# Layer 0's experts on sorted tokens: rows fetched by indirect DMA, weights addressed from a register

## The chip, the core and the metric

The kernel runs on one core of a Trainium2 chip. The metric is the device time of one execution in microseconds. A core has TensorE (PE, with its weight loads shown apart as PEld), VectorE (DVE), ScalarE (ACT), GpSimd (POOL) and SyncE (SP), which here only issues transfers; the transfers of all queues run on 16 DMA engines.

## What is computed

The reference is a decoder of two layers on 32 sequences of 128 tokens with 128 features, all float32. Layer 0 has a time-mixing block, self attention and cross attention with 16 heads of 64, a feed-forward with 512 hidden features, and a mixture of experts; layer 1 has an attention, a cross attention with a mask, and a second mixture of experts with a capacity. Each block's output goes through a layer normalization. The change is about layer 0's experts:

```
t = x * rsqrt(mean(x*x) + 1e-6) * norm_weight
gate_logits = t @ gate_w.T                       # 8 experts
gate_scores, expert_idx = top_k(gate_logits, 2)
routing_weights = softmax(gate_scores)
combine = zeros(T, 8).at[arange(T)[:, None], expert_idx].add(routing_weights)
for each expert (W1, B1, W2, B2, c = its column of combine):
    acc += c[:, None] * (gelu(t @ W1.T + B1) @ W2.T + B2)    # 128 -> 256 -> 128
out = x + acc
```

Every token thus uses two of the eight experts; the other six have a weight of zero. The layer's result is the normalization of x + out.

## The kernel before

The 4,096 tokens are cut into eight groups of 512 (G = 4 sequences). Between layers a group's rows go out to DRAM and come back (`putx`, `getx`, L174 to L186). Each layer is written as units, and `build` (L1361) places every piece of work at a time measured in units; `pipeline` sorts the pieces by that time, and the framework then orders each engine's instructions from this list by a simulated timeline of its own. `SHIFT`, `AHEAD`, `FC`, `L5`, `L6` and so on (L26 to L57) are those due times. Layer 0's cross attention runs from unit 64 to 135, the feed-forward (`fc_parts`, L527) of a group starts eleven units ahead of its experts, the experts run from unit 132 to 203, and layer 1's attention starts at unit 172.

Buffers are shared by tag (`BUFS` and `TAG`, L34 to L40): a tag has a few slots, and all uses that name it, of whatever layer, take turns in them. So `x` has four slots, `xs` four, `cs` five, `res` two, `pt` four, `e` six. PSUM's eight banks are shared in the same way (`BANKS`).

The experts (`moe_units`, L629) treat a group as a whole, with no regard to the choice of experts. `pre` normalizes the rows (Square on ScalarE, L642; the power on POOL, L646; scaling on VectorE, L648), transposes them and splits the result into a high and a low part (L652, L653). `route` computes the logits, the two best experts as one-hot rows (`top2`, L571) and the weights. `hid(e)` multiplies all 512 tokens with expert e's first matrix, as three rounded products for each half (`mm3`, L149, recorded at L152 to L154) and a Gelu (L694). `outp(e)` multiplies with the second matrix in plain float32 (L705) and adds the result, times the token's weight for this expert, to an accumulator on VectorE (L708). `turn_c` and `post` add the second biases by one small matmul a sequence (L680, L714, L717). All weights stay in SBUF (`moe_w`, L618).

Beside the experts run the loads for layer 1's experts: `presplit` (L1128) takes a slab through one staging buffer (SP's load at L1134, a cast on ScalarE at L126, a subtraction on POOL at L127) and writes it back from POOL's queue (L1136). Layer 1's attention has its own work on POOL (`rope` at L865, `parts3` at L739 to L742), on VectorE (L862, L903) and on ScalarE (L930).

Of the kernel before, what the change touches and what calls it, by code (L numbers as in the profile page):

```python
# [9 lines left out]
F32 = mybir.dt.float32  # L10
FR = mybir.dt.float32r
# [11 lines left out]
G = 4  # L23
GT = G * 128

SHIFT = {1: 0, 2: 0, 3: 4, 4: 0, 5: -24, 6: 8, 7: 0}  # L26
# [10 lines left out]
           mt="res", acc="xb", ct8="msk", mh="v", mres="res", parts="qk", stack="big", ob="v", ax="cs", at="pt", ar="pt",  # L37
           ap="e", ok="pt", ares="cs", oT="v", xwo="pt", mi="xb", m="msk", cx="xs", cc="v", xt="pt", xr="v", xp="e",
           xres="cs", pre="big", turn="xs", turnw="v", kT="xs", kh="x", kl="cs", hot="xs", d="big", w="e", hh="e", hl="qk",
           w2="pt", eo="big", kres="v", mx0="xs", mx1="cs", s0="msk", s1="xb", x="x")  # L40
# [3 lines left out]
            oproj="mm", fc1="mm", fc2="S", logits="mm", logitsT="PT", cT="PT", hid="mm", outp="S", b2="PT", bank="PV",  # L44
# [10 lines left out]

AHEAD = {2: 8, 3: 32, 4: 24, 5: 20, 6: 40, 7: 164}
# [13 lines left out]
class Net:  # L70
# [546 lines left out]

    def moe_w(self):  # L618
        w = {}
        w["w1"] = [self.split_slab("moe_w1", i * 1024) for i in range(2)]  # L620
        w["w2"] = None
        w["b1"] = self.col("moe_b1", 16)
        w["nw"] = self.col("moe_nw", 1)
        w["g"] = self.gate_w("moe_gate")
        w["b2"] = self.cst.tile([8, 128], F32, name="moe_b2")
        self.nc.sync.dma_start(out=w["b2"], in_=self.a["moe_b2"])
        return w

    def moe_units(self, g, getw, done):  # L629
        nc, sm = self.nc, self.sm  # L630
        w = Later(getw)
        st = {}

        def load():
            st["x"] = self.getx(g)

        def pre():
# [9 lines left out]
            for b in range(G):  # L647
                nc.vector.tensor_scalar(t[:, b, :], x[:, b, :], rs[:, b:b + 1], None, ALU.mult)  # L648
            tp = self.xT_ps(t)
            th = self.t("mx1" if g % 2 else "mx0", dt=FR)  # L650
            tl = self.t("mx1" if g % 2 else "mx0", dt=FR)
            nc.scalar.activation(th, tp, AF.Copy, scale=w["nw"])  # L652
            nc.vector.scalar_tensor_tensor(tl, tp, w["nw"], th.bitcast(F32), ALU.mult, ALU.subtract)  # L653
            st["t"] = th, tl
            acc = self.tok("acc")
            nc.gpsimd.tensor_tensor(acc, x, x, ALU.add)
            st["acc"] = acc

        def route():
            lg = sm.tile([128, G, 8], F32, name="lg")  # L660
            self.logits(w["g"], *st["t"], lg)
            (o1, o2), (m1, m2) = self.top2(lg)
            d = sm.tile([128, G], F32, name="d")
            nc.vector.tensor_tensor(d, m1, m2, ALU.subtract)
            th = sm.tile([128, G], F32, name="th")
            nc.scalar.activation(th, d, AF.Tanh, scale=0.5)
            p = sm.tile([128, 2, G], F32, name="p")
# [869 lines left out]
```

## Time and profile before

| what | us |
|---|---|
| median of 2 runs | 1868.26 (1867.07 to 1869.44) |
| profiled execution, its own time | 1872.84 |
| its span in the profile | 1871.1 |
| ScalarE busy, 670 to 940 us | 195.52 of 270 |
| VectorE busy, 940 to 1243 us | 211.84 of 303 |
| TensorE busy, 1600 to 1871 us | 244.29 of 271 |

A group of instructions is shown as: line, engine, operation, output and input by name, shapes and count, then busy time and the mean ns of one, then the engine's idle time ahead of them and what ended it. Since matmuls overlap, the mean of one is longer than the step from one to the next; the steps are read from the chain of waits, which lists the work that ended last in order of time. The profile takes one execution; times beside each other are compared within it, and the medians between kernels.

### The profile page before, as it was taken

Reading aid. Unit: us, or ns where it says so; the run is one execution under the profiler, and the core shown is the slowest. Engines: PE = TensorE matmul, PEld = TensorE weight load, DVE = VectorE, ACT = ScalarE, POOL = GpSimd, SP = SyncE. Lnnn points to the kernel's source line nnn. Section 1 sums busy time; section 2 is a strip of 40 time slices with the busy share of each in tenths; the row PEclk is TensorE's granted clock in tenths of the full one; section 3 lists DMA queues with packets and bytes.
Section 4 is the critical chain, followed back from the end, with each engine's and each line's share of the span. In section 5 each row is a group of like instructions: output and inputs, shape, how many; then the busy total and the mean of one; then the engine's idle time right before and its main releaser. Section 6 shows DMA issues by size and latency. Waiting matters only on the chain.

```text
span 1871.1 us, 44846 instructions
## 1 busy us (share of the span) xinstructions
PE 1728.4 (92%) x15658; PEld 1400.8 (75%) x15658; DVE 1383.4 (74%) x5256; ACT 1177.4 (63%) x3703; POOL 863.3 (46%) x1201
## 2 busy tenths in 40 slices
PE   5899999989999999999999999999779888898998
PEld 3677777777778788887788888866556555688888
DVE  7978888776766676666776677677655767789896
ACT  2776766768777777777645554346666646556654
POOL 4655555564544444444434444245432432246555
PEclk7999999999999999999999999999998989899999
DMA  5101101010110000100133435468979988222222
GB/s 158 36 31 40 39 20 41 31 53 26 48 48 26 20 13 25 42 8 12 57 119 123 164 134 130 109 179 198 200 191 225 217 197 205 73 81 92 96 90 70
DMA packets 148770, 171.45 MB, mean 92 GB/s; under 512 B 13128, under 2 KB 100176, under 8 KB 146064
## 3 DMA queue, kind: packets, MB, share of 16 engines
q1 hardware_dynamic: 145808, 154.95, 31.0%
q0 software_dynamic: 1584, 11.54, 1.5%
q8 instruction: 124, 2.03, 0.5%
q10 hardware_dynamic: 1152, 2.10, 0.3%
q14 instruction: 102, 0.84, 0.1%
HBM read 114.81 MB, written 55.31 MB: 91 GB/s over the span
## 4 chain that ended last, share of the span: by engine, by line
PE 62%; DVE 18%; ACT 6%; DMA 5%; POOL 4%; issue 3%; SPq 1%; POOLq 0%; ACTq 0%; DVEq 0%
PE mm L489 6%; PE S L705 6%; PE mm L152 6%; PE mm L153 5%; PE mm L154 5%; PE PV L169 4%; PE PT L452 4%; PE S L169 3%; DVE e L432 3%; PE PV L164 3%; PE PT L1283 3%; ACT e L437 2%; DMA x<-x 2%; PE S L164 2%; PE S L554 2%
## 5 line engine op out<-in xcount | busy, mean ns | idle before, releaser
L437 ACT ACTIVATE e<-e,nm 128x128 f32<-128x128 f32 x1024 | 397.6, 391 | 108.5 <-POOL nm L434 106.4
L441 POOL TENSOR_TENSOR e<-e,ri 128x512 f32<-128x512 f32 x256 | 266.1, 1044 | 205.0 <-DVE ri L439 185.7
L432 DVE CUSTOM_DVE_ANT_0 e<-S,msk 128x128 f32<-128x128 f32 x1024 | 228.7, 284 | 21.5 <-PE PT L452 12.8
L437 ACT ACTIVATION_READ_ACCUMULATOR e<-e,nm 128x1 f32 x1024 | 193.1, 189 | 0.0
L452 PE MATMUL PT<-ident,e 128*128 128x128 f32 x1024 | 150.8, 278 | 6.8 <-ACT v L397 4.6
L169 PE MATMUL S<-qk 64*128 64x128 f32 x1792 | 148.5, 280 | 0.0
L169 PE MATMUL PV<-pt,v 128*64 128x128 f32 x1792 | 141.1, 277 | 0.0
L452 PEld LDWEIGHTS PT<-ident,e 128*128 128x128 f32 x1024 | 115.6, 141 | 32.7 <-issue 8.7
L694 ACT ACTIVATE v<-mm,col_moe_b 128x512 f32<-128x512 f32 x128 | 85.5, 685 | 81.8 <-PE mm L154 81.3
L705 PEld LDWEIGHTS S<-w,v 128*128 128x128 f32 x1024 | 128.6, 191 | 7.8
L705 PE MATMUL S<-w,v 128*128 128x128 f32 x1024 | 133.7, 276 | 0.0
L152 PE MATMUL mm<-xs,w 128*128 128x512 f32 x296 | 127.2, 441 | 4.7 <-DVE qk L409 1.9
L489 PE MATMUL mm<-w,big 128*128 128x128 f32 x1024 | 127.6, 278 | 0.0
L489 PEld LDWEIGHTS mm<-w,big 128*128 128x128 f32 x1024 | 120.9, 192 | 7.6 <-issue 5.0
L439 DVE RECIPROCAL ri<-su 128x4 f32<-128x4 f32 x256 | 43.4, 173 | 110.7 <-ACT e L437 106.4
L169 PEld LDWEIGHTS S<-qk 64*128 64x128 f32 x1792 | 123.9, 188 | 0.4 <-DVE x L220 0.4
L153 PE MATMUL mm<-xs,w 128*128 128x512 f32 x296 | 118.9, 402 | 1.6 <-DVE xs L146 1.6
L434 POOL TENSOR_SCALAR nm<-mx 128x4 f32<-128x4 f32 x256 | 58.6, 233 | 133.1 <-DVE mx L432 119.5
L154 PE MATMUL mm<-xs,w 128*128 128x512 f32 x296 | 118.4, 400 | 0.0
L230 POOL TENSOR_SCALAR rsqv<-bmv 128x4 f32<-128x4 f32 (+1 forms) x73 | 14.4, 197 | 214.4 <-DVE bmv L203 197.7
L454 ACT COPY pt<-PT 128x512 f32<-128x512 f32 x128 | 74.3, 581 | 59.5 <-PE PT L452 58.8
L169 PEld LDWEIGHTS PV<-pt,v 128*64 128x64 f32 x1792 | 108.7, 137 | 2.3 <-issue 2.2
(324 smaller groups left out, 5052.1 us busy)
## 6 DMA issues: line engine op xcount, KB each, us to landing
x<-x SPq DMA_DIRECT2D x151, 256.0 KB
big<-d_st SPq DMA_DIRECT2D x52, 512.0 KB
pt<-d_w SPq DMA_DIRECT2D x64, 256.0 KB
d_st<-qk SPq DMA_DIRECT2D x48, 256.0 KB
d_st<-qk SPq DMA_DIRECT2D x16, 768.0 KB
d_w<-big POOLq DMA_DIRECT2D x11, 1024.0 KB, 5.1
w<-d_w SPq DMA_DIRECT2D x7, 1024.0 KB
w<-d_st SPq DMA_DIRECT2D x12, 512.0 KB
```

What stands on the lines that cost most here:

```text
L152: mm(out=out, lhsT=wh, rhs=xh, start=True, stop=False)
L153: mm(out=out, lhsT=wh, rhs=xl, start=False, stop=False)
L154: mm(out=out, lhsT=wl, rhs=xh, start=False, stop=True)
L164: i = mm(out=out, lhsT=w, rhs=x, **more)
L169: i = mm(out=out, lhsT=w, rhs=x, **more)
L432: self.seen = nc.vector.tensor_tensor_reduce(e[:, t], s[h][:, t], msk[:, t], 1.0, NEG, ALU.add, ALU.max, mx[:, b:b + 1])
L437: nc.scalar.activation(e[:, t], e[:, t], AF.Exp, bias=nm[:, b:b + 1], scale=0.125, accum_out=su[:, b:b + 1])
L441: nc.gpsimd.tensor_tensor(e3, e3, ri.unsqueeze(2).to_broadcast([128, G, 128]), ALU.mult)
L452: nc.tensor.transpose(pt[:, t], es[h][:, t], self.ident)
L489: nc.tensor.matmul(out=o[:, b, :], lhsT=st["ot", p // 4][:, p % 4, b * 128:(b + 1) * 128], rhs=w["wo"][:, p * 128:(p + 1) * 128], start=p ...
L694: nc.scalar.activation(h, hp, AF.Gelu, bias=w["b1"][:, k:k + 1])
L705: nc.tensor.matmul(out=o[:, b, :], lhsT=hs[i][:, b * 128:(b + 1) * 128], rhs=w["w2"][:, k * 128:k * 128 + 128], start=i == 0, stop=i == 1)
```

## The change

The experts now work on two waves of four groups (GW = 4, 2,048 tokens, NT = 16 blocks of 128). For each group `pre` also writes the normalized rows to a DRAM table `td`. When a wave's four groups are through, `route` finds the two experts of each token for the whole wave, counts with a scan and three small matmuls how many tokens each expert has, and gives every (token, choice) a slot in a list sorted by expert, in which each expert starts at a multiple of 256. `invert` turns the slots into a list of token numbers by 32 pairs of one-hot comparisons on VectorE and 32 matmuls. The list has NS = 23 tiles of 256 slots, enough for any routing; `ei` holds the expert of each tile.

Then, for each pair of tiles, `fetch` gathers rows from `td` by four indirect DMAs on POOL and `turn` transposes them. `wload` reads a tile's expert number into a register of SP and loads that expert's weights and biases (642 columns) from DRAM into a ring of three buffers. `hid` and `outp` work on the 256 rows in plain float32, and the results go to a table `yd`. At the end `again` gathers the two result rows of every token by eight indirect DMAs a group, and `combine` adds them with their weights to 2x before the normalization. The due times change: the feed-forward's groups have their own list `FCAT` and stand at units 92 to 142, among the cross attention; layer 1's attention starts at unit 150.

```diff
-SHIFT = {1: 0, 2: 0, 3: 4, 4: 0, 5: -24, 6: 8, 7: 0}
+SHIFT = {1: 0, 2: 0, 3: 4, 4: 0, 5: -46, 6: 8, 7: 0}
...
-           mt="res", acc="xb", ct8="msk", mh="v", mres="res", parts="qk", stack="big", ob="v", ax="cs", at="pt", ar="pt",
+           mt="res", acc="xb", ct8="msk", mh="v", y4="e", yg="pt", parts="qk", stack="big", ob="v", ax="cs", at="pt", ar="pt",
...
+GW = 4
+NT = GW * G
+NS = NT + 7
+EW = 642
+RING = 3
+
+FCAT = (92, 97, 102, 107, 113, 120, 128, 136)
+QAT = (132, 154)
+QSTEP = 1.0
+AHEADW = 0.85 * QSTEP
...
     def moe_w(self):
...
-        w["w1"] = [self.split_slab("moe_w1", i * 1024) for i in range(2)]
-        w["w2"] = None
-        w["b1"] = self.col("moe_b1", 16)
+        t = self.w8()
+        w["ring"] = [t[:, i * EW:(i + 1) * EW] for i in range(RING)]
+        t = self.w8()
+        w["xT"] = [t[:, i * GT:i * GT + GT] for i in range(2)]
...
+            nc.sync.dma_start(out=rows(td)[:, i * G:(i + 1) * G, :], in_=t)
             tp = self.xT_ps(t)
...
+            nc.vector.tensor_tensor_scan(fl(s), w["run"], fl(m), 0.0, ALU.mult, ALU.add)
+            cp = self.pst("slots")
...
+            nc.tensor.matmul(out=cnt, lhsT=w["tri"], rhs=m[:, :, 1:], start=True, stop=False)
+            nc.tensor.matmul(out=cnt, lhsT=w["ones"], rhs=s[:, :, 0:NT], start=False, stop=True)
+            nc.tensor.matmul(out=n, lhsT=w["ones"], rhs=s[:, :, NT], start=True, stop=True)
...
+        def invert(part, parts):
...
+            for k in range(part * n, (part + 1) * n):
+                z, i = k % 2, k // 2
+                ah, bh = a4[:, k % n * 128:k % n * 128 + 128], b4[:, k % n * 2 * NS:(k % n + 1) * 2 * NS]
+                nc.vector.tensor_scalar(ah, w["lane"], tf[:, 1, z, i:i + 1], None, ALU.is_equal)
+                nc.vector.tensor_scalar(bh, w["tile"], tf[:, 0, z, i:i + 1], w["id"][:, i:i + 1], ALU.is_equal, ALU.mult)
+                nc.tensor.matmul(out=st["ip"], lhsT=ah, rhs=bh, start=k == 0, stop=k == 2 * NT - 1)
...
+        def fetch(q):
+            x = st["x4", q] = self.tok("x")
+            for k in range(2 * len(tiles(q))):
+                nc.gpsimd.indirect_dma_start(x[:, k, :], None, td,
+                                             bass.IndirectOffsetOnAxis(ap=st["ix"][:, q * 4 + k:q * 4 + k + 1], axis=0))
...
+        def wload(j):
+            t = st["w", j] = w["ring"][(wv * NS + j) % RING]
+            e = nc.values_load(st["ei"][0:1, j:j + 1], engines=[mybir.EngineType.SP], min_val=0, max_val=7,
+                               skip_runtime_bounds_check_because="the sum of eight comparisons, at most 7")
+            nc.sync.dma_start(out=t, in_=self.a["moe_e"][bass.ds(e, 1)].rearrange("e p c -> p (e c)"))
+
+        def hid(j):
...
+            x = st["xT", j // 2][:, j % 2 * 256:j % 2 * 256 + 256]
+            for f in range(2):
+                o = hp[:, f * 256:f * 256 + 256]
+                nc.tensor.matmul(out=o, lhsT=t[:, f * 128:f * 128 + 128], rhs=x, start=True, stop=True)
+                nc.scalar.activation(h[:, f, :], o, AF.Gelu, bias=t[:, 512 + f:513 + f])
+
+        def outp(j):
...
+            for k in range(2):
+                for f in range(2):
+                    nc.tensor.matmul(out=o[:, k, :], lhsT=h[:, f, k * 128:k * 128 + 128],
+                                     rhs=t[:, 256 + f * 128:384 + f * 128], start=f == 0, stop=f == 1)
...
+            nc.vector.tensor_tensor(y, o, t[:, 514:642].unsqueeze(1).to_broadcast([128, 2, 128]), ALU.add)
+            nc.sync.dma_start(out=rows(yd)[:, j * 2:j * 2 + 2, :], in_=y)
+
+        def again(i):
...
+                for z in range(2):
+                    nc.gpsimd.indirect_dma_start(y[z][:, b, :], None, yd, bass.IndirectOffsetOnAxis(
+                        ap=st["si"][:, z, i * G + b:i * G + b + 1], axis=0))
...
+        u = [(last + 9.5, route)]
+        for i in range(GW):
+            u += [(FCAT[g0 + i] + 7, lambda i=i: load(i)), (FCAT[g0 + i] + 8, lambda i=i: pre(i))]
+        for k in range(8):
+            u.append((last + 10.5 + k * 0.3, lambda k=k: invert(k, 8)))
+        for q in range(Q):
+            at = QAT[wv] + q * QSTEP
+            u += [(at - 2.5, lambda q=q: fetch(q)), (at - 0.2, lambda q=q: turn(q))]
+        for j in range(NS):
+            at = QAT[wv] + j / 2 * QSTEP
+            u += [(at - AHEADW, lambda j=j: wload(j)), (at, lambda j=j: hid(j)),
+                  (at + 0.6 * QSTEP, lambda j=j: outp(j))]
+        end = QAT[wv] + Q * QSTEP + 0.5
+        for i in range(GW):
+            u += [(end + i, lambda i=i: again(i)), (end + i + 1.5, lambda i=i: combine(i)), (end + i + 2.5, lambda i=i: post(i))]
```

## The prediction

> **What bounds the kernel now.** I read the page's first part for the span, then the windows by stage, then the chain of waits inside the experts' stage, then the groups of instructions and SP's waits.
>
> ```profile
> span 1871.1 us, 44846 instructions
> ...
> PE 1728.4 (92%) x15658; PEld 1400.8 (75%) x15658; DVE 1383.4 (74%) x5256; ACT 1177.4 (63%) x3703; POOL 863.3 (46%) x1201
> ```
>
> TensorE is busy for 92% of the span; no other engine is near it. The windows (PE, PEld, DVE, ACT and POOL busy, granted clock, DMA share, GB/s) say where:
>
> ```profile
> 670.00:940.00 270.00, 264.58 (x2358) 217.95 (x2359) 188.14 (x965) 195.52 (x748) 119.99 (x181) 1.00 0.09 28
> 940.00:1243.00 303.00, 296.73 (x2130) 259.82 (x2130) 211.84 (x776) 141.24 (x279) 121.80 (x178) 1.00 0.46 133
> 1243.00:1600.00 357.00, 304.51 (x4273) 203.84 (x4269) 245.51 (x588) 215.53 (x467) 136.02 (x168) 0.92 0.83 199
> ```
>
> The first is the second half of layer 0's cross attention (stage A), the second the experts with the feed-forward (stage B), the third layer 1's two attentions (stage C). In A and B TensorE is 98% busy, in C 85% beside a DMA share of 0.83. So work taken off TensorE in B is worth its full time, as long as something is ready to follow. The chain inside B (start, us, what) is TensorE alone:
>
> ```profile
> 1002.25 1.78 PE S L705 x16
> 1004.03 0.23 PE mm L152
> 1004.26 0.23 PE mm L153
> 1004.50 0.23 PE mm L154
> 1004.73 0.23 PE mm L152
> 1004.95 0.23 PE mm L153
> 1005.18 0.23 PE mm L154
> 1005.41 1.78 PE S L705 x16
> ```
>
> One expert for 512 tokens takes 3.16 us: six 128x512 matmuls at 0.23 and eight float32 128x128 matmuls (two records each) at 1.78/8 = 0.22. These steps are durations on the path; the means of the groups overlap and are longer.
>
> **Removed from TensorE.** Eight groups by eight experts, 64 x 3.16 = 202 us. The bias matmuls of L714 and the transposes of L680, 8 x (1.08 + 0.44) = 12 us, where 1.08 and 0.44 are what the chain gives for eight such records and for four transposes. Sum 214 us.
>
> **Added to TensorE.** There are two waves with 23 tiles of 256 rows, 46 tiles whatever the routing: 11,776 rows instead of 32,768. A tile has two float32 matmuls of 256 columns and four of 128. By twice the 0.22 a wide one is 0.445; the far row is the 128x512 float32 projection, 0.56 a record, which halves to 0.56 a call. I take the nearer 0.445: 4 x 0.22 + 2 x 0.445 = 1.78 a tile, 82 us (to 93). Transposes of fetched rows: 92 x 0.11 = 10. The sort's 64 small matmuls at the 0.11 of a 128x128 step: 7, and six count matmuls 1. Sum 100 us. TensorE saves 114 us, and 103 at the upper price. With every hole filled the span would be 1757.
>
> **Stage A pays.** The feed-forward moves from units 121 and later to 92 and later. About 4.5 more groups of it (12 x 0.23 + 16 x 0.22 + four transposes = 6.8 each), as many preparations for the routing (1.3 each) and wave 0's sort (4) move into A: 41 us of TensorE, no loss in itself, as B gives it back. VectorE there gets 4.5 x (10.4 for the three normalizations' and residuals' rows + 2.1), 10 for some 49 routing instructions at the 0.17 to 0.2 of the 128x32 rows, and 32 x (0.28 + 0.17) = 14 for the inverted list: 188 + 56 + 24 = 268 of 311 us, 86%. The nearest stretch with that load is 50 to 400 us, where VectorE is 83% busy and TensorE 94%, against 98% in A now. 311 / 0.937 - 311 / 0.98 = 15 us lost; bounds 0 and 40 (the latter if shared buffers, `res` with two and `xs` with four, hold attention up as well).
>
> ScalarE must now change between Exp and Gelu inside A. The change has a row:
>
> ```profile
> L548 ACT ACT_TABLE_LOAD x2 | 2.6, 1283 | 0.0
> L694 ACT ACTIVATE v<-mm,col_moe_b 128x512 f32<-128x512 f32 x128 | 85.5, 685 | 81.8 <-PE mm L154 81.3
> L1136 POOL DMA_DIRECT2D d_w<-big x11 | 7.0, 640 | 3.3 <-POOL big L127 3.3
> ```
>
> Six groups with one excursion each, there and back, are 12 x 1.28 = 15 us; with four each, 62. ScalarE goes from 195.5 to 240 (287) of 311: it still has room, so I charge nothing beyond the 15 us above. The cover is ScalarE's idle quarter; gone, each excursion costs its 2.6 us.
>
> [...]
>
> **Stage B pays in two ways.** First, a gap ahead of wave 1. Its routing needs the last feed-forward group, which follows the last attention group. From its last logits to its first expert I count routing 10, some hops between engines 3, inversion 14, four indirect DMAs on POOL, landing 3 (a 256 KB row load shows 2.7 in the chain), transposes and ScalarE 1.5: about 37 us. TensorE then has the tail of wave 0 and the sort's own matmuls, some 12 us; layer 1 waits for wave 0's combined rows, which themselves need eight gathers for each group. Gap 25 us; bounds 0 (layer 1's work is moved up) and 40.
>
> Second, the pace of the experts. A pair of tiles is 3.56 + 0.44 = 4.0 us of TensorE, with 0.8 of other work between (layer 1's projections or the last feed-forward): 4.8. POOL issues four indirect DMAs for a pair. No row shows one. The nearest is L1136, a plain DMA on POOL with as many partitions, 0.64 us a piece; that is the lower end, since the new ones read an index for each row too. The upper end is four times that, 2.4. I take twice, 1.2: one such issue for the addresses and one for the descriptors. With layer 1's 9.8 us of POOL work (L865, L739 to L742) over eight units, 1.2 a unit, POOL needs 4 x 1.2 + 1.2 = 6.0 a pair. The weights give a near number: three buffers, each held for two tiles (3.56), the bias add (0.45), then the 329 KB load with its register read (4.5 from the 256 KB landing of 2.7 to 3.8): 8.5 / 3 = 2.8 a tile, 5.7 a pair. So POOL sets the pace, 6.0 against 4.8, over 23 pairs 28 us.
>
> [...]
>
> VectorE in B and beyond: gone are L708's 72 us and about 37 of routing and residuals; added are two sorts (48), 46 bias adds (20) and 64 combines (22). That evens out and lies beside TensorE. SP loses nothing by count, but its 46 weight loads, eight stores of normalized rows and 46 stores of results stand in a queue that already waits:
>
> ```profile
> SPq L186 <- DVE x L217: 49.7, 6, 16.5
> SPq L1134 <- POOL big L127: 42.3, 18, 3.9
> SPq L1134 <- DMA wst<-in_m_w_dram: 29.7, 13, 2.8
> ```
>
> **Stage C.** Layer 1 starts 22 units earlier but overlaps the experts by 19 units instead of 31: some 26 us of its TensorE work move from a 98% to an 85% stage, 4 us. The bytes of the weights (15 MB) and rows (18 MB) fall into B, where the share is 0.46; bound 0 to 20.
>
> **Sum.** -114 + 15 + 25 + 28 + 4 = -42. The profiled execution took 1872.84, 1.7 over its span; the median shown is 1868.26, so 1868 - 42 = 1826, 2.3% less.
>
> **Rivals.**
> 1. The holes are filled: layer 1's work stands in the gap and POOL's issue costs the 0.64 of L1136. Then only A's 15 us remain: 1868 - 114 + 15 = 1769. For it: the timeline at 1230 to 1245 already mixes matmuls of both layers. Against it: layer 1 waits for wave 0's gathers.
> 2. The queue eats it: the weight load goes out less than one tile ahead on SP, which waits 72 us for L1134 here, about 2.3 a time. If half of the 46 loads come 1.6 us late, 37 more: 1863. For it: L186 waits up to 16.5 us. Against it: the first half of the presplit's loads now fall before the experts.
> 3. Slower: POOL's indirect DMA is dear. A pair then takes 4t + 1.2, and 23 x (4t + 1.2 - 4.8) eats the 114 - 15 - 25 - 4 = 70 that are left at t = 1.66 us. At 2.4 the pace costs 138, the gap 5 more: 1868 - 114 + 15 + 30 + 138 + 4 = 1941. For it: the index of every row must be read. Against it: L1136.
>
> **How the numbers follow.** A measurement of this kernel tells about 2% from no change. Forecast 0.40 (own range 1795 to 1850, about 0.33 of it under 1831), rival 1 0.10, rival 2 0.28, rival 3 0.22 (0.06 of it still below 1906). Faster 0.33 + 0.10 = 0.43; same 0.07 + 0.28 + 0.06 = 0.41; slower 0.16. The range 1770 to 1925 leaves out about half of rival 1 and the dear half of rival 3.
>
> **What would show it.** TensorE busy near 1615 us (right for the 114); the first window near 325 long; the indirect DMA's row on POOL at 1.2 us, and 156 of them; PE waiting for the fetched tile or for DMA into `w`, some 28 us over both waves, and one hole near 25 us ahead of wave 1; 12 more table loads. Wrong if POOL's row is over 1.66 us, if SP's waits grow ahead of the weight loads, or if the first window grows past 350.

## The result, and the profile after

The changed kernel takes 2067.62 us (median of 2 runs, 2066.64 to 2068.61) against 1868.26: 1.107 times as long, with a 95% interval of 1.102 to 1.112. The forecast was 1826, its range ended at 1925. The profiled execution took 2068.61, 2.1 over its span.

From the page of the changed kernel:

```profile
span 2066.5 us, 43698 instructions
...
PE 1686.4 (82%) x14874; PEld 1340.2 (65%) x14874; DVE 1391.6 (67%) x5194; ACT 1172.0 (57%) x3699; POOL 999.4 (48%) x1347
```

TensorE has less to do, but it is busy for 82% of the span instead of 92%. The losses can be placed by two landmarks: the last Exp of layer 0's attention (start 916.0 before, 1045.1 after) and the last maximum that layer 1's attention takes (1386.4 before, 1577.5 after). Each is the end of "first and last start" in the first row that the trace gives for that line. So stage A became 129 us longer, stage B from Exp to maximum 62 (470 to 532), and the rest 4 (484.7 to 489.0). The three windows of the prediction, moved by these landmarks (same columns: PE, PEld, DVE, ACT, POOL busy, granted clock, DMA share, GB/s):

```profile
670.00:1069.00 399.00, 335.46 (x2581) 268.47 (x2579) 266.04 (x1231) 248.55 (x830) 173.78 (x283) 0.91 0.18 59
1069.00:1434.00 365.00, 189.68 (x1067) 150.29 (x1067) 142.97 (x436) 80.36 (x171) 205.91 (x223) 0.71 0.61 163
1434.00:1791.00 357.00, 292.61 (x4236) 196.21 (x4229) 239.73 (x573) 213.91 (x464) 133.92 (x165) 0.94 0.83 197
```

In A TensorE falls from 98% to 84% busy, in B from 98% to 52%, and the granted clock there from 1.00 to 0.71. No other engine is full either (POOL, at 56% in B, is the nearest): B is now made of chains. Four windows inside it are wave 0's experts, a hole, wave 1's experts, and a second hole (the first two tiles of wave 1 start at 1241.0 and 1242.4, the third only at 1255.1, and what held it back the profile does not name; so the first hole's window has 14 us of wave 1 in it):

```profile
1055.00:1171.00 116.00, 83.09 (x473) 69.80 (x473) 35.70 (x118) 42.55 (x96) 58.57 (x65) 0.85 0.72 204
1171.00:1255.00 84.00, 21.93 (x93) 18.01 (x92) 48.56 (x186) 6.89 (x13) 61.15 (x65) 0.58 0.39 121
1255.00:1348.00 93.00, 62.29 (x337) 50.27 (x337) 16.02 (x36) 28.63 (x59) 42.73 (x46) 0.88 0.68 171
1348.00:1430.00 82.00, 27.90 (x180) 17.13 (x181) 48.16 (x121) 4.65 (x9) 53.41 (x59) 0.51 0.58 137
```

The two holes leave TensorE idle for 62 and 54 us. Whom it waits for, first in the hole ahead of wave 1, then in the one behind it (us in total, times, longest):

```profile
PE PT L201 <- DMA x<-x: 26.1, 1, 26.1
PE PT L759 <- DVE bh L758: 13.4, 5, 4.7
...
PE PT L201 <- DMA x<-x: 26.3, 1, 26.3
PE mm L179 <- DVE pt L983: 14.6, 1, 14.6
```

L201 is the transpose with which layer 1's attention begins a group, and its rows come only when the whole wave is through and gathered back. L759 is the matmul of the inverted list, waiting for its one-hot comparisons. In TensorE's order L201 stands behind wave 1's sort and ahead of its experts:

```profile
1206.12 1.05 PE L759 MATMUL PT<-bh,xs 128*128 128x46 f32 x4 [1.13 <-DVE bh L758]
1233.23 1.09 PE L201 MATMUL PT<-ident,x 128*128 128x128 f32 x4 [26.06 <-DMA x<-x]
```

POOL's timeline shows the gathers, and what queues behind them:

```profile
1177.39 1.04 POOL L817 DMA_INDIRECT pt<-yd,si  x1 [0.17 <-issue]
...
1205.11 0.94 POOL L817 DMA_INDIRECT pt<-yd,si  x1 [0.30 <-issue]
1206.36 0.94 POOL L817 DMA_INDIRECT pt<-yd,si  x1 [0.30 <-issue]
...
1221.17 0.98 POOL L817 DMA_INDIRECT pt<-yd,si  x1 [0.30 <-issue]
...
1233.16 1.06 POOL L770 DMA_INDIRECT x<-td,ix  x1 [2.34 <-issue]
```

A start every 1.25 us where no other work lies between, 32 of them between 1177 and 1222. The list of wave 1 was ready at 1207.4 (L762 on VectorE), but its first fetch goes out at 1233: POOL is at the gathers until 1222, and then at normalizations (L240, L242) and the presplit's subtraction (L137). The fetches' row on the page, and the table loads from 650 to 1100 us:

```profile
L770 POOL DMA_INDIRECT x<-td,ix x92 | 88.3, 960 | 49.2 <-issue 26.3
...
L558 ACT ACT_TABLE_LOAD x11 | 14.1, 1283 | 0.2
L447 ACT ACT_TABLE_LOAD x10 | 12.8, 1283 | 0.2
```

An indirect DMA holds POOL for 0.96 us and 0.30 pass to the next. The 21 table loads are 27 us of ScalarE, where the kernel before has three loads.

Stage A has a chain through POOL that the prediction did not have:

```profile
1015.09 0.20 POOL L670 TENSOR_SCALAR rsqv<-ss 128x4 f32<-128x4 f32 x1
1015.56 0.98 POOL L770 DMA_INDIRECT x<-td,ix  x1 [0.27 <-issue]
...
1021.83 0.95 POOL L770 DMA_INDIRECT x<-td,ix  x1 [0.30 <-issue]
1022.81 1.27 POOL L549 TENSOR_TENSOR v<-x,row_fc_b 128x512 f32<-128x512 f32 x1
1024.04 0.20 POOL L444 TENSOR_SCALAR nm<-mx 128x4 f32<-128x4 f32 x1
1024.19 1.05 POOL L672 TENSOR_TENSOR rsq<-rsqv,mhalf 128x4 f32<-128x4 f32 x1
```

L670 and L672 are the two halves of one group's normalization ahead of the routing; six of wave 0's fetches stand between them in POOL's order, and the softmax's L444 waits behind as well. TensorE's timeline has the other end:

```profile
1027.97 1.12 PE L201 MATMUL PT<-ident,res 128*128 128x128 f32 x4 [13.93 <-DVE res L674]
```

It sat 13.9 us for the scaled rows (L674) that need L672. SP's waits, which the prediction watched: the first two lines are the rows of a group going out over the whole run, before (L186) and after (L196); the last is from 1050 to 1350 us, the store of an expert's result, which stands ahead of later weight loads.

```profile
SPq L186 <- DVE ri L439: 305.4, 12, 49.3
```

```profile
SPq L196 <- DVE ri L449: 263.4, 14, 37.3
...
SPq L809 <- DVE e L808: 38.0, 16, 6.2
```

Over the whole run SP does not stand longer for that wait than before (the prediction's 49.7 and 42.3 us are waits from 940 to 1243 us, the experts' stage). The 38.0 us at the stores are new; what they cost by holding later loads up, a run below tries.

### The profile page after: what moved, and what is told of

It is laid out like the page before. It is cut to its first block, busy times and chain, and to the rows that moved or that the text cites. A ratio compares the mean times of both kernels' runs of the same rounds, so it can differ in the third digit from the quotient of the medians.

```text
span 2066.5 us, 43698 instructions
## 1 busy us (share of the span) xinstructions
PE 1686.4 (82%) x14874; PEld 1340.2 (65%) x14874; DVE 1391.6 (67%) x5194; ACT 1172.0 (57%) x3699; POOL 999.4 (48%) x1347
## 4 chain that ended last, share of the span: by engine, by line
PE 23%; DVE 11%; DMA 9%; issue 6%; POOL 5%; ACT 5%; SPq 2%; POOLq 0%; ACTq 0%; DVEq 0%
DMA x<-x 4%; PE PT L1404 2%; PE mm L162 2%; DMA w<-in_moe_e_dram 2%; DVE x L227 2%; POOL pt L817 1%; PE PV L174 1%; PE PV L179 1%; PE mm L163 1%; PE mm L164 1%; PE mm L795 1%; ACT e L447 1%; PE PT L1207 1%; PE mm L499 1%; PE S L179 1%
## 5 line engine op out<-in xcount | busy, mean ns | idle before, releaser
L499 PE MATMUL mm<-w,big 128*128 128x128 f32 x1024 | 132.1, 284 | 3.2 <-ACT big L558 3.2
L499 PEld LDWEIGHTS mm<-w,big 128*128 128x128 f32 x1024 | 125.7, 198 | 10.9 <-issue 4.5
L444 POOL TENSOR_SCALAR nm<-mx 128x4 f32<-128x4 f32 x256 | 59.0, 234 | 135.6 <-DVE mx L442 124.0
L240 POOL TENSOR_SCALAR rsqv<-bmv 128x4 f32<-128x4 f32 (+1 forms) x73 | 14.6, 200 | 206.9 <-DVE bmv L213 203.7
L770 POOL DMA_INDIRECT x<-td,ix x92 | 88.3, 960 | 49.2 <-issue 26.3
L162 PE MATMUL mm<-xs,w 128*128 128x512 f32 x232 | 101.1, 452 | 8.6 <-ACT big L558 6.2
L795 PE MATMUL mm<-w,w 128*128 128x256 f32 x184 | 65.4, 445 | 49.6 <-issue 26.2
L930 ACT COPY v<-PV 128x256 f32<-128x256 f32 x128 | 48.0, 375 | 98.0 <-PE PV L179 96.1
L808 DVE TENSOR_TENSOR e<-S,w 128x256 f32<-128x256 f32 x46 | 19.4, 421 | 124.5 <-PE S L803 82.2
L419 DVE COPY qk<-mm 128x512 f32<-128x512 f32 x128 | 86.5, 677 | 22.1 <-PE S L179 12.3
```

The lines of the kernel that those rows point to most:

```text
L162: mm(out=out, lhsT=wh, rhs=xh, start=True, stop=False)
L419: nc.vector.tensor_copy(kt, kp)
L444: nc.gpsimd.tensor_scalar(nm, mx, -0.125, 0.0, ALU.mult, ALU.add)
L499: nc.tensor.matmul(out=o[:, b, :], lhsT=st["ot", p // 4][:, p % 4, b * 128:(b + 1) * 128], rhs=w["wo"][:, p * 128:(p + 1) * 128], start=p ...
L770: nc.gpsimd.indirect_dma_start(x[:, k, :], None, td, bass.IndirectOffsetOnAxis(ap=st["ix"][:, q * 4 + k:q * 4 + k + 1], axis=0))
L795: nc.tensor.matmul(out=o, lhsT=t[:, f * 128:f * 128 + 128], rhs=x, start=True, stop=True)
```

## The experiments

The theory after the result: the saved TensorE time is real, and is lost to separate chains (table switches and POOL's order in A; sort, gathers, weights and the waves' order in B). The rivals were the prediction's own (POOL's price sets the pace; the queue of weights eats it) and "one cause seen several times". Each time has beside it the kernel before on the same chip, which took 1859 to 1869; so prices below are taken from ratios: 1.1067 less the run's ratio, times 1868. Runs with an interval are given it; the others are one execution, and where a kernel ran two or three times its times spread by up to 13 us. The two landmarks are those of the profiled executions as they stand: that of the kernel before took 1872.84, 0.2 to 0.7% more than the ones beside the runs, so at the landmarks differences of some 2 to 10 us can be the chip's. For the experts' waves below, a wave goes from the first matmul of its experts to the last (L795 and L803 in the changed kernel), and the gap lies between the two waves: there they take 116, 69 and 106 us.

| run | us | before beside it | last Exp | last maximum |
|---|---|---|---|---|
| before | 1868 | | 916 | 1386 |
| after | 2068 | | 1045 | 1578 |
| feed-forward early only | 1931.7 | 1863.6 | 967 | 1439 |
| Tanh | 2023.9 | 1863.6 | 1024 | 1534 |
| plain DMAs | 1974.8 | 1863.6 | 1030 | 1488 |
| no sort | 2012.4 | 1863.6 | 1025 | 1518 |
| weights once | 2020.7 | 1859.2 | 1042 | 1534 |
| Tanh, plain, no sort | 1898.3 | 1859.2 | 989 | 1414 |
| reordered | 2071.4 | 1859.2 | 1024 | 1578 |
| filled holes | 2063.8 | 1859.2 | 1044 | 1570 |
| plain for results only | 2033.1 | 1864.0 | 1042 | 1535 |
| feed-forward early, Tanh | 1921.2 | 1864.0 | 961 | 1433 |
| stores later | 2076.2 | 1864.0 | 1044 | 1581 |
| all four taken | 1868.7 | 1864.0 | 988 | 1376 |
| all four, reordered | 1868.7 | 1864.9 | 986 | 1381 |
| plain, reordered | 1961.2 | 1864.9 | 1026 | 1474 |
| one excursion | 2070.9 | 1864.9 | 1043 | 1575 |
| all four, no barrier | 1841.1 | 1869.2 | 990 | 1354 |

**The move of the feed-forward alone**, in the kernel before:

```diff
-            ahead(u - AHEAD[3], lambda: load(3))
+            ahead(FCAT[0] - 8, lambda: load(3))
...
-                    place([[(0, f)]], max(u + 8 * g + i, 0) if on(2) else u + 8 * g + i + 11)
+                    place([[(0, f)]], FCAT[g] + i + 11)
```

> The kernel before, with nothing changed but the units of layer 0's feed-forward, which stand where the changed kernel has them. Theory (the move itself is dear: stage A was 98% full on TensorE, and each excursion from Exp to Gelu holds attention's softmax up): the last Exp of layer 0 comes 60 to 100 us later than in the kernel before, of which 31 to 41 are moved work that the experts' stage gives back, and the kernel takes 1895 to 1930. Forecast of the prediction (15 us lost): near 1883. Rival (A grew by the sort alone): 1865 to 1875, and the last Exp only 31 to 41 later.

1931.7, 1.036 times the kernel before (1.033 to 1.039): 67 us lost with no sort, gather or address in the kernel. The theory's range for the time was missed by 2 us, and its 60 to 100 us for the last Exp by 9: it comes 51 us later, 31 of it the moved work (4.5 groups at 6.8), so A loses 20, near the 15 of the prediction. But B stays at 471 us, although 31 us of work left it. Its windows and, from 970 to 1075, TensorE's waits:

```profile
950.00:1000.00 50.00, 38.60 (x307) 31.98 (x307) 25.89 (x123) 24.63 (x81) 16.34 (x23) 0.90 0.14 49
1000.00:1050.00 50.00, 35.92 (x218) 30.45 (x217) 21.43 (x87) 18.07 (x36) 19.49 (x49) 0.83 0.33 119
```

```profile
PE PT L192 <- DVE res L649: 10.1, 2, 5.1
PE PT L192 <- DMA x<-x: 7.3, 1, 7.3
```

Where attention ends, TensorE waits for residuals and rows of single groups. The reading is that the feed-forward had filled such gaps among the experts and is now used up; no run tests it by itself.

**Tanh in the feed-forward** (from 650 to 1100 us this run has one table load, the changed kernel 21):

```diff
-            nc.scalar.activation(st["h"][:, f, :], hp, AF.Gelu, bias=w["b1"][:, f:f+1])
+            nc.scalar.activation(st["h"][:, f, :], hp, AF.Tanh, bias=w["b1"][:, f:f+1])
```

> The changed kernel with Tanh in place of Gelu in layer 0's feed-forward, so that ScalarE needs no other table there than Exp's (the feed-forward computes another function). Theory: of the 21 table loads in stage A nearly all go, 27 us of ScalarE, and with the stalls behind them 25 to 45 us of the time: 2020 to 2045. Rival (ScalarE had a quarter of its time free, so the loads are covered, as the prediction had it but for 15 us): 2053 to 2070.

2023.9, as the theory had it: 39 us by the ratios. The last Exp comes 21 us sooner. ScalarE's free quarter does not cover the loads.

**Plain DMAs in place of the indirect ones**:

```diff
-            for k in range(2 * len(tiles(q))):
-                nc.gpsimd.indirect_dma_start(x[:, k, :], None, td,
-                                             bass.IndirectOffsetOnAxis(ap=st["ix"][:, q * 4 + k:q * 4 + k + 1], axis=0))
+            i = nc.sync.dma_start(out=x[:, 0:n, :], in_=rows(td)[:, lo:lo + n, :])
...
-                    nc.gpsimd.indirect_dma_start(y[z][:, b, :], None, yd, bass.IndirectOffsetOnAxis(
-                        ap=st["si"][:, z, i * G + b:i * G + b + 1], axis=0))
+                nc.sync.dma_start(out=y[z], in_=rows(yd)[:, lo:lo + G, :])
```

> The changed kernel with plain DMAs on SP in place of the 156 indirect ones (one for four: the rows are fetched in their order, so the experts get other tokens than their own; sort, waits on the list, weights and tiles stay). Theory (POOL's gathers, 1.25 us each and in one order with all other work on POOL, make the two holes between the waves and slow the pairs): 70 to 120 us less, 1950 to 2000. Rival (the holes are the chain of dependences from the last feed-forward group through the sort to the experts, and the wave's barrier, whoever moves the rows): 10 to 40 less, 2030 to 2058. Rival of the prediction (POOL sets the pace of the pairs only): about 28 less, near 2040, with the pairs of both waves faster.

1974.8, inside the theory's range: 88 us, the largest single price. The gap ahead of wave 1 shrinks from 69 to 56 us, and what TensorE waits for in it is now the routing and the sort. Its waits from 1140 to 1198, and the first from 1198 to 1288 (L797 is the experts' first matmul here):

```profile
PE PT L712 <- DVE cs L706: 17.4, 1, 17.4
PE PT L759 <- DVE bh L758: 9.4, 8, 4.3
...
PE mm L797 <- DMA w<-in_moe_e_dram: 16.2, 14, 3.1
```

Both waves get shorter, 116 to 99 and 106 to 90 us. But in wave 1 all of that is in its first three tiles: the last twenty take 79.9 us as before, 8.0 a pair, with TensorE waiting for weights. So the rival of the prediction, that POOL sets the pace of the pairs, does not hold there. The last Exp comes 15 us sooner.

**No sort**: `route` and `invert` replaced by constants.

```diff
-            lg = w["lg"]
...
+            si = st["si"] = small("si", [2, NT], I32, 2)
+            nc.gpsimd.iota(si, [[2048, 2], [128, NT]], base=0, channel_multiplier=1)
...
-                nc.vector.tensor_copy(ix, st.pop("ip"))
+                nc.gpsimd.iota(ix[:, 0:32], [[0, 2], [128, NT]], base=0, channel_multiplier=1)
```

> The changed kernel without the sort: routing's counts and the inverted list are left out, and the lists of rows, slots and experts are constants of the same sizes (two tokens' weights 0.5; the indirect DMAs, the weights by address and all tiles stay). Theory: VectorE's burst of 35 us near the end of stage A and 20 us of the hole ahead of wave 1 go: 30 to 70 us less, 2000 to 2038. Rival (the sort lies beside POOL's gathers and other waits): within 15 of 2068. Rival (the sort is most of the loss): under 1960.

2012.4, 50 us, by the theory. From 1135 to 1205 TensorE now has one wait:

```profile
PE PT L201 <- DMA x<-x: 58.8, 1, 58.8
```

So without the gathers the sort makes this hole, and without the sort the gathers do (gaps of 56 and 68 us, against 69 with both): two chains lie beside each other in it, and neither edit alone closes it. The 50 us are elsewhere: the last Exp comes 20 us sooner, and the waves take 100 and 85 us in place of 116 and 106. Why they do is not separated (fetched rows now lie in order, and VectorE has less to do).

**Weights once**: the register reads and 43 of 46 loads are dropped.

```diff
-            e = nc.values_load(st["ei"][0:1, j:j + 1], engines=[mybir.EngineType.SP], min_val=0, max_val=7,
...
-            nc.sync.dma_start(out=t, in_=self.a["moe_e"][bass.ds(e, 1)].rearrange("e p c -> p (e c)"))
+            if wv * NS + j < RING:
+                nc.sync.dma_start(out=t, in_=self.a["moe_e"][j:j + 1].rearrange("e p c -> p (e c)"))
```

> The changed kernel with the experts' weights loaded into the three ring buffers once; the 43 later loads and all reads of an address into a register are left out (later tiles use wrong weights). Theory: TensorE's waits for these loads, 7 us in wave 0 and 10 in wave 1, go, and with them part of the 38 us that SP stands at the stores of results ahead of the loads: 15 to 45 less, 2023 to 2053. Rival (the loads and SP's order set the pace of the pairs, 8 to 9.4 us against 4.8 of TensorE work): 70 or more less, under 1998. Rival (covered by POOL's pace): 2058 or more.

2020.7, 2 us beyond the theory's range; by the ratios 37 us. The two waves and the hole between them:

```profile
1053.00:1133.00 80.00, 68.41 (x451) 59.69 (x450) 30.79 (x108) 36.34 (x80) 51.91 (x57) 0.94 0.60 164
1133.00:1227.00 94.00, 22.95 (x80) 16.02 (x78) 56.10 (x195) 10.44 (x24) 59.83 (x66) 0.53 0.40 133
1227.00:1297.00 70.00, 59.53 (x359) 51.90 (x359) 16.35 (x37) 30.20 (x63) 47.41 (x51) 0.92 0.57 126
```

From first to last matmul the waves go from 116 and 106 us to 81 and 72, and the gap grows from 69 to 93, so of 69 us 45 are left. The last twenty tiles of wave 1 take 61.9 us in place of 79.9: it is the weights that set the pace of the pairs there. In wave 1 TensorE now waits for fetched rows (1227 to 1297):

```profile
PE PT L778 <- DMA x<-td,ix: 9.2, 10, 1.6
```

**Tanh, plain DMAs and no sort together** (the three edits above):

> The changed kernel with the three edits of the runs before together: Tanh in the feed-forward, plain DMAs on SP for rows, no sort (other function, other rows, constant lists). Singly they took 44, 93 and 55 us off 2068. Theory (three causes in different places, of which sort and gathers share the hole ahead of wave 1): about additive or a little more, 1840 to 1880: without them the change would be worth nothing to 25 us, since the move of the feed-forward costs some 20 to 40 and the waves' barriers remain. Rival (they are one cause seen thrice): 1940 or more. Rival (they are all that stands against the 114 us): 1760 to 1800.

1898.3: 160 us by the ratios, against 177 for the three prices added. They are nearly separate; the time lies between the theory's range and the rival of one cause, nearer to the theory.

**Another written order**:

```diff
-SHIFT = {1: 0, 2: 0, 3: 4, 4: 0, 5: -46, 6: 8, 7: 0}
+SHIFT = {1: 0, 2: 0, 3: 4, 4: 0, 5: -39, 6: 8, 7: 0}
...
-QAT = (132, 154)
+QAT = (138, 151.2)
...
-        end = QAT[wv] + Q * QSTEP + 0.5
+        end = (152.2, QAT[1] + Q * QSTEP + 0.5)[wv]
+            d = 2 * i
```

> The changed kernel with other places in the written order, all work kept: wave 0 starts 6 units later, so that wave 1's sort lies beside wave 0's experts; wave 1's first fetches stand ahead of wave 0's gathers on POOL, and these are spread over wave 1; layer 1 starts 7 units later. Theory (the hole ahead of wave 1 is made by the order: sort behind the last experts, fetches behind 32 gathers): the hole of 85 us shrinks to under 30, and the kernel takes 1990 to 2035. Rival (the hole only moves: to the end of the feed-forward's chain ahead of wave 0, and behind wave 1 where layer 1 waits): 2050 to 2080.

2071.4, ratio 1.114 (1.103 to 1.125): no gain, the rival is right. The hole ahead of wave 1 does close (its first matmul comes 9 us after wave 0's last). But POOL then runs 64 indirect DMAs almost without a pause from 1186 to 1270, and in wave 1 TensorE stands 39 us at layer 1's first rows. Its waits from 1195 to 1300:

```profile
PE PT L201 <- DMA x<-x: 39.2, 1, 39.2
PE mm L795 <- DMA w<-in_moe_e_dram: 9.7, 6, 2.5
PE PT L778 <- DMA x<-td,ix: 6.2, 6, 2.3
```

**Holes filled with idle matmuls**:

```diff
+            if i == 0:
+                t = self.pst("inv").rearrange("p (b s) -> p b s", s=128)
+                for _ in range(100):
+                    nc.tensor.matmul(out=t, lhsT=self.identb, rhs=self.identb.unsqueeze(1).to_broadcast([128, 4, 128]),
+                                     start=True, stop=True)
```

> The changed kernel with 100 bf16 matmuls of 128x512, whose result nobody reads, on TensorE ahead of each wave's gathers (200 in all, 0.22 us each at full clock, 44 us), so that TensorE is not idle in the two long holes. Theory (the clock granted, 0.5 to 0.7 in and behind the holes, is lowered by the idle time itself): the clock there is near 1, what follows runs faster, and the kernel takes 2035 to 2060. Rival (the clock follows something else, or the stretches behind the holes wait for other engines and a faster TensorE is worth nothing): 2065 to 2115.

2063.8, ratio 1.110 (1.101 to 1.119), no difference from the change itself, and between the two ranges. The first hundred ran from 1159 to 1181, at the start of its hole; the second from 1307 to 1343, beside wave 1's last tiles, so the second hole got none. Its windows still show a clock of 0.70 and 0.56, so the run does not settle what a clock kept up throughout would be worth:

```profile
1157.00:1234.00 77.00, 40.56 (x177) 24.77 (x175) 47.67 (x188) 5.83 (x12) 50.55 (x56) 0.70 0.39 129
...
1340.00:1400.00 60.00, 15.57 (x93) 9.63 (x92) 31.82 (x92) 0.85 (x2) 40.31 (x44) 0.56 0.45 105
```

It shows something else: 200 more matmuls, 44 us at the 0.22 each of the first hundred (78 in a row in 17.0 us), cost the kernel nothing where they stood.

**Plain DMAs for the results only** (the second part of the edit above):

> The changed kernel with plain DMAs on SP (two for a group) in place of the 64 indirect ones that bring the experts' results back to their tokens; the 92 that fetch rows stay (results come back in their slots' order, so tokens get other rows). Theory (the 32 gathers of a wave, 40 us of POOL in one piece, hold wave 1's fetches and layer 1 back; the fetches themselves are mostly hidden by a pair's 8 to 9 us): most of the 93 us that all 156 cost together, 55 to 80 less, 1988 to 2013. Rival (the pace of the pairs, 5 us of fetches each, is the price): under 40 less, 2028 or more.

2033.1: 30 us of the 88, the rival's number. The theory, that the gathers of results are most of it, falls; the 92 fetches and the two kinds together make the rest. The gap ahead of wave 1 goes from 69 to 52 us; the last Exp (1042) and the waves (114 and 116 us) hardly change for the better, so what plain DMAs gained in A and in the waves belongs mostly to the fetches.

**The early feed-forward with Tanh**, in the kernel before (the two edits above):

> The kernel before with the feed-forward moved early, as in the first run (1932 there), and Tanh in place of Gelu in it. Theory (two causes: 19 table loads, 24 us of ScalarE in a stage where the softmax is on the way; and holes at the end of the feed-forward, where its chain of normalizations no longer stands beside experts): the first goes, 15 to 30 less than 1932, 1902 to 1917 (some 4 less on a chip that runs the kernel before at 1859). Rival (all of the loss is table switching): 1865 to 1890. Rival (none of it): 1925 to 1932.

1921.2, 10 us better by the ratios than with Gelu, between the theory's range and the rival that expects nothing. So of the 67 us that the move alone costs, the switches are a small part, and one execution does not give it closely. In the changed kernel the same edit is worth 39: the price of a load depends on the kernel around it.

**Stores of results later in SP's queue**:

```diff
-                  (at + 0.6 * QSTEP, lambda j=j: outp(j))]
+                  (at + 0.6 * QSTEP, lambda j=j: outp(j)), (at + 1.4 * QSTEP, lambda j=j: stor(j))]
```

> The changed kernel with each store of an expert's result written 0.8 of a pair later in SP's queue, behind two more weight loads, so that SP need not stand at it (38 us in wave 0 and wave 1) before it sends the next weights; nothing else differs. Theory (the pairs' 8 to 9 us come from weights sent late by SP's order): 15 to 35 less, 2030 to 2055. Rival (the loads themselves, 329 KB each through three buffers, are the pace): 2058 to 2075.

2076.2: no gain. SP now stands just as long at the weight loads themselves (L786), for the same bias add (from 1050 to 1350):

```profile
SPq L786 <- DVE e L808: 39.2, 18, 5.1
```

L808 is the last to read a tile's weights, and the load three tiles later takes the same buffer. So the weights are late by the ring of three buffers and by their loads, not by SP standing at the stores.

**All four taken away**:

> The changed kernel with all four taken away at once: Tanh in the feed-forward, plain DMAs for rows and results, no sort, weights loaded once (three of them took 1898 together; the weights alone 47 off 2068). Theory (a fourth separate cause): 1840 to 1870, at the time of the kernel before, so that nothing of the 114 us would be seen even then: what remains is the move of the feed-forward, the barriers of two waves and the clock. Rival (with all four gone TensorE's saving shows): under 1810. Rival (weights are covered by then): 1885 to 1900.

1868.7 beside 1864.0, as the theory had it. From its page:

```profile
PE 1627.5 (87%) x14798; PEld 1303.3 (70%) x14798; DVE 1323.2 (71%) x4968; ACT 1142.0 (61%) x3677; POOL 848.0 (45%) x1199
```

TensorE has 101 us less to do than before, in a span only 4 us shorter: 97 us became idle time, most of it in a hole of 42 us between the waves and one behind them. Its waits from 1060 to 1260:

```profile
PE PT L201 <- DMA x<-x: 16.1, 2, 12.7
PE mm L162 <- DVE pt L915: 12.9, 3, 11.2
PE PT L201 <- DVE res L674: 11.7, 2, 10.9
```

**All four taken away, and reordered**:

> The kernel of the run with all four taken away (1869; Tanh, plain DMAs, no sort, weights once), with the written order of the reordered run (wave 0 six units later, wave 0's results brought back in between wave 1's experts, layer 1 seven units later). Theory (the last part is the order itself: two holes of 43 and about 35 us in which TensorE's next instruction waits for a wave to be complete): the hole ahead of wave 1 closes, since POOL no longer refills it, and 25 to 60 go: 1810 to 1845, the first time under the kernel before. Rival (the hole moves behind wave 1 whatever POOL does): 1860 to 1885.

1868.7 again, the rival. Wave 1 follows wave 0 without a hole, but a new one opens ahead of wave 0, where L674 is waited for. From 985 to 1260:

```profile
PE PT L201 <- DVE res L674: 21.8, 4, 15.8
PE PT L201 <- DMA x<-x: 19.0, 2, 13.5
PE mm L162 <- DVE pt L916: 12.8, 5, 10.5
```

**Plain DMAs, and reordered**:

> The changed kernel with plain DMAs on SP for rows and results (1975) and the written order of the reordered run (2071 with POOL's indirect DMAs, where the order changed nothing). Theory (the order could not help there because POOL, 70 indirect DMAs in one piece of 87 us, was the limit): with POOL free the order helps, 25 to 60 less than 1975, 1915 to 1950. Rival (the sort's and the weights' chains hold the waves apart in any order): 1960 to 1990.

1961.2, 15 us better than unreordered by the ratios, at the edge of the rival's range and 11 short of the theory's. With POOL's indirect DMAs the same order gained nothing, so POOL is at most a part of what kept it from helping.

**One excursion to Gelu for a group**:

```diff
-        return [load, pre] + [lambda f=f: (fc1(f), fc1(f + 1)) for f in (0, 2)] + [fc2, post,
+        return [load, pre] + [lambda: [fc1(f) for f in range(4)], lambda: None] + [fc2, post,
```

> The changed kernel with the four first matmul blocks of a feed-forward group, and so its four Gelus, written in one unit in place of two, nothing else: some 5 fewer switches there and back, about 10 table loads, 13 us of ScalarE. Theory (the switches hold the softmax up; all of them cost 44): 12 to 25 less, 2043 to 2056. Rival (four Gelus in a row hold the softmax up as much as a switch does, or TensorE waits for a buffer): 2060 to 2075.

2070.9, ratio 1.111 (1.107 to 1.115). It decides nothing: the trace still has 21 loads from 650 to 1100, so the switches that the edit was to remove are still there.

**All four taken away, and the wave no barrier**:

```diff
-SHIFT = {1: 0, 2: 0, 3: 4, 4: 0, 5: -46, 6: 8, 7: 0}
+SHIFT = {1: 0, 2: 0, 3: 4, 4: 0, 5: -50, 6: 8, 7: 0}
...
-        td = self.dp.tile([GW * GT, 128], F32, name=f"td{wv}")
+        td = [self.dp.tile([GT, 128], F32, name=f"td{wv}_{i}") for i in range(GW)]
...
+                nc.sync.dma_start(out=y[z], in_=rows(yd[z * GW + i]))
...
-        end = QAT[wv] + Q * QSTEP + 0.5
+        end = QAT[wv] + 5.7
```

> The kernel of the run with all four taken away (1869), in which a pair of tiles now waits for the rows of its own group alone (four arrays of rows and twelve of results for a wave in place of one of each), a group's results are brought back as soon as its two pairs are done, six units earlier than before, and layer 1 starts four units earlier. Theory (what is left of the loss is the wave as a barrier: all four groups must be there before any expert, and all experts done before any row of layer 1, so that TensorE's saving turns into two holes which reordering only moves): both holes shrink and 30 to 70 go, 1800 to 1840, under the kernel before. Rival (the holes are layer 1's own chain and its shared buffers, not the wave): 1855 to 1880.

1841.1 beside 1869.2 (ratio 0.985): 28 us better than with the barrier, 33 by the ratios, the first time under the kernel before, 1 us above the theory's range and 14 under the rival's. The edit changes three things at once (whom a pair waits for, when results come back, when layer 1 starts), and the results that are brought back are those of the first eight of a wave's twelve pairs, so nothing waits for the other four. The barrier with these due times is worth the 33 us; the barrier alone was not tried, and a true kernel, whose tokens can lie in any pair, could not drop it so. The gap between the waves shrinks from 42 to 32 us only. TensorE's longest wait from 1060 to 1260 is now for the scaled rows of wave 1's own groups:

```profile
PE PT L201 <- DVE res L674: 17.5, 1, 17.5
```

A still ends 74 us later than before. B, from the last Exp to the last maximum, is 365 us, 106 less than before.

## Why the prediction was wrong, step by step

**What bounds the kernel: right.** TensorE did, and that is why nothing else was watched closely enough.

**Removed 214, added 100: right.** With all four taken away and no barrier, TensorE is busy for 1619 us, 109 less than before, to which the 8 of the sort's matmuls are to be added back: 101, near the 103 of the prediction's upper price. The changed kernel's own 1686 has a mean clock of 0.91 beside it (0.955 there, 0.97 before), so part of its busy time is put down to the lower clock: in the first hole, at 0.54 (1225 to 1241 us), a 128x512 matmul takes 0.43 us to the next (L163 at 1236.43, L164 at 1236.86), where the prediction's chain has 0.23 at 1.00.

**Stage A, 15 us lost: the step that failed first.** The forecast was 41 of moved work and 15 lost; measured are 129, so 88 lost. The 15 were about right for the feed-forward alone (20). Missing were wave 0's sort (in the sum only with its 4 us of TensorE and as VectorE load), its fetches and the switches, worth 20, 15 and 21 us of the last Exp when taken away singly, 57 together. The step counted engines' busy shares. But the normalization's power (L672) and the softmax's L444 queue on POOL behind fetches, and the table loads stand on ScalarE between the softmax's Exps. No share of busy time shows that. The prediction named the window's growth past 350 us as its sign of failure; it grew to 399.

**ScalarE's twelve switches, cover a free quarter: wrong in cover.** There were 21 loads in place of three, 27 us of ScalarE. Tanh took 20 of them away, 26 us busy, and the kernel gained 39 (one execution). The prediction had 12 loads, 15 us of ScalarE, and charged nothing for them. The load's 1.28 us was right.

**Gap ahead of wave 1, 25 us (0 to 40): wrong.** 62 us idle. The chain of the sort was counted (37 us; the list is ready 36 us after wave 0's last matmul), but wave 0's 32 gathers, 38 us at the prediction's own 1.2 each, were not set ahead of wave 1's fetches in POOL's queue. With plain DMAs for the results the gap is 17 us shorter. A second hole of the same make, 54 us idle behind wave 1, was not in the sum at all: all eight groups' first rows of layer 1 come only from a finished wave.

**The pace, 6.0 a pair: price right, bound wrong.** An indirect DMA was taken at 1.2 and takes 1.25 from start to start. It holds POOL for 0.96 us for 128 rows; one issue for the addresses and one for the descriptors was the author's estimate, and no run shows how the 0.96 us divides. From first to last matmul the pairs took 116 / 11.5 = 10.1 and 106 / 11.5 = 9.2 us. The last twenty tiles of wave 1 show what sets the pace: 8.0 us a pair in the changed kernel, 8.0 with plain DMAs, 6.2 with the weights once, 5.6 with all four taken away (the other runs in this order that load the weights have 7.2 to 8.9, and 9.8 where the fillers stand in that stretch). So the term that was mis-sized is the weights' ring, put at 5.7 a pair. In those twenty tiles a load goes out 1.4 us after the bias add that frees its buffer, the tile's first matmul comes 5.0 us after that, and its own bias add ends 5.9 us later: 12.3 / 3 = 4.1 us a tile, where the prediction had 8.5 / 3 = 2.8. This is rival 2's cause, the weights, but not its mechanism: later stores in SP's queue did nothing. What the first tiles of each wave lose, where wave 0 and the fetches share POOL, is not taken apart.

These three make up B: it was forecast at -102 (the sum's -114 + 25 + 28, less the 41 that move to A) and came to +62. By the windows above, gap 62 - 25 = 37, second hole 54, waves 209 - 138 = 71: 162 of 164.

**Stage C, 4 us: right** (4.3).

**The rivals.** Rival 3 had the right sign for another reason: its point of decision was 1.66 us an indirect DMA, and the price stayed below. Every rival changed one price in a full pipeline. That the pipeline itself would come apart, with holes that are refilled from the next chain when one is closed, was none of them, and the 2068 lies outside the range for that. The prices found singly (39, 88, 50 and 37) add up to 214; together they are 195, and only the last run, 33 more, brings the kernel below where it began.

**Left open.** What the lower clock in the holes costs by itself: the fillers did not cover the holes. What the wave's barrier costs alone. And what of A's remaining 74 us is the moved work: the prediction's count would be 37 without the sort, but no run took the move back from the changed kernel.

## What to carry to other kernels

When work leaves the bounding engine, ask what that work was covering: here, as far as the runs show, the dense experts hid the chains of normalization, routing and layer change, and the waves of four groups took the cover away. Write out, for each engine, the order of its instructions at the moment a stage begins, and put the issues of the stage before into it at their price (here 32 gathers at 1.25 us on POOL, ahead of wave 1's first fetch). A low busy share was no cover here where the instruction stood in a chain that TensorE waited for: ScalarE was 62% busy in A, and taking 20 of its table loads away was worth 39 us.

## What the hardware showed

- Indirect DMAs on POOL, 128 rows of 512 bytes each: 0.96 us busy and 0.30 to the next, for results nearly the same (0.98), and at most 1.42 us in the hole where VectorE was 58% busy.
- In the stretches where TensorE is a quarter to a third busy the granted clock is 0.58 and 0.51, and 0.85 to 0.88 in the waves beside them (TensorE 72% and 67% busy); before, it was 1.00 in the experts' stage (98% busy). What lowers it no run here shows, nor whether a higher clock behind the holes would save time: the 44 us of fillers left most of the holes idle.
- The load of 1.28 us for an activation table stayed the same in 21 places, while its price in the kernel's time was 10 us for 18 loads taken away in one kernel and 39 for 20 in the other (one execution each).
